# Phi by half sequences on array quarters, attention's first two tiles joined, and new ranks for the planner

## The chip, the cores and the metric

The kernel runs on one core of one Trainium2 chip. The metric is the device time of one execution in microseconds (us); lower is better. The time of the kernel before is the median of three runs, 779.21 us (779.11 to 779.4). Everything is computed in float32.

## What is computed

A transformer block over 32 sequences of 512 tokens with 256 features. The first half is an attention whose queries and keys are the same feature vector phi; the second half routes each token to the best 8 of 64 slots, updates the slots by a gated step, and reads them back. Cut to what matters:

```python
x  = x + attn(layernorm(x));  x = x + slots(layernorm(x))
# attn, per token of one sequence
q      = tanh(x @ W_charge.T + b)                    # one number per token
shell  = normalise(x @ W_shell.T + b_shell)          # 64
proj   = shell @ omega.T + rff_bias                  # 32
phi_s  = [cos(proj), sin(proj)] * scale              # 64
phi    = sum_m mag[m] * q**m * (phi_s @ W_combine[m].T)     # m = 0..4, 64 numbers
logits = phi @ phi.T * exp(-0.03 * |i - j|) / temp,  causal
out    = softmax(logits) @ (x @ W_v.T + b_v) @ W_out.T + b_out
# slots
alpha  = softmax of the 8 largest of 64 route logits, 0 elsewhere
slot   = gated step of (alpha.T @ x / sum(alpha)),  out = alpha @ (slot @ wv.T) @ wo.T
```

The decay is split into a factor that grows with the query's place (`dec_q`) and one that falls with the key's (`dec_k`), so phi is multiplied by each once and the logits come from one matrix product.

## The kernel before, in words

The work is cut into 16 groups of `GB = 2` sequences. A group has `GT = 8` tiles of 128 tokens, and its input tile `x` lies in one of five buffers. Each group passes four stages, which the code writes as functions.

- `features`: transposes of `x` (`pta`, L698), the joint projection to shell, charge and values (`pf`, L732, evicted to `sv` by L745), charges repeated over 64 columns (`qrep`, L768, GpSimd) and transposed (`ptq`), shells normalised and transposed (`pts`). The angles come from one full-array matrix product with a block-diagonal 128x128 `om` (`pp`, L858; eviction L865). After rounding (L872, L873) and the sine (L880) the powers `tp[m]` are built by multiplying with q or q squared (L891; m = 1 and 3 on VectorE, 2 and 4 on GpSimd). In `tp`, partitions 0 to 63 hold sequence 0 and 64 to 127 sequence 1, with all 512 tokens along the free axis.
- phi, the end of `features`: a 64x64 quarter of the array reads one half of the partitions and writes one half. Powers 0, 3 and 4 go through the two diagonal quarters (`STRAIGHT`, L930). Powers 1 and 2 go through the other two (`SWAPPED`, L941), and so must first stand on the other half of partitions: four DMA transfers per group on SP's queue copy `tp` to `tps` (L915). The three PE steps are chained: powers 0 and 1, then 3 and 2, then 4 alone, which occupies two quarters. Each of two PSUM banks then holds part of both sequences: ScalarE copies one bank (`both`, L958), VectorE adds the other (L962), and `dec_q` is multiplied on by VectorE (L970), `dec_k` by GpSimd (L977).
- `attention`: for each of four query tiles i, the logits of width (i+1)*128 for both sequences on the two row halves of the array (`pl`, L996), the masked minimum on VectorE (L1014), the exponential with its sum on ScalarE (L1026), the reciprocal (L1042), transposes (`ptp`, L1052), their eviction (`prT`, L1078), the product with the values (`po`, L1056), and the sum into `x` (L1065).
- `router` and `slots`: layer norm (statistics L662; the small GpSimd steps L673 to L683; application L1096), transposes `ptb`, hidden layer `ph` (L1122), logits `prr` (L1147, the two column halves of the array), transposes `prt`, eight `max`/`match_replace` pairs (L1178, L1179), the exponential (L1196), the weights `al` (L1212, GpSimd), the slots' input `psi` (L1235, column halves), the gates `prz` and `pn` (L1284), the new values `pv` (L1371), and the outputs `py` (L1391, row halves), added to `x` (L1405) and stored.

Engines take their instructions in the order in which they are emitted. That order is made by a planner (class `Plan`): each step has an engine, a cost in us, the steps it needs and the buffers it uses. `order` places the step that could start first by these costs, and among equal starts the one with the lowest rank. A rank is `g * STRIDE + (earliest time inside its group) + DELAY[stage]`. An activation table that must be loaded adds `TABLE`. The tile pools' sizes are in `SLOTS_OF`: eight PSUM banks `ps`, one `phi`, and one `tp`.

```python
STRIDE = 28.0
DELAY = {"setup": 0.0, "features": -12.0, "attention": -3.0, "router": 15.0, "slots": 15.0}
```

Of the kernel before, what the change touches and what calls it, by code (L numbers as in the profile page):

```python
# [15 lines left out]
P = 128  # L16
D = 256
KD = D // P
T = 512
NT = T // P  # L20
# [6 lines left out]
STRAIGHT, SWAPPED = (0, 3, 4), (1, 2)  # L27
# [43 lines left out]
STRIDE = 28.0  # L71

DELAY = {"setup": 0.0, "features": -12.0, "attention": -3.0, "router": 15.0, "slots": 15.0}
# [24 lines left out]
class Plan:  # L98
# [8 lines left out]
    def add(self, eng, cost, emit, after=(), uses=(), table=None, land=0.0, rank=None, spare=0):  # L107
        s = Step(eng, cost, emit, [a for a in after if a], list(uses), rank, table, land)
        s.spare = spare
        s.g, s.stage = self.group, self.stage  # L110
        for u in s.uses:
            u.users += 1
        for a in s.after:
            a.next.append(s)
        s.waits = len(s.after)
        self.steps.append(s)
        return s

    def order(self):
# [17 lines left out]
        table = None  # L137
# [6 lines left out]
        while len(placed) < len(self.steps):  # L144
            best = None
            for e, todo in ready.items():
                for s in todo:
# [13 lines left out]
                    if s.table and s.table != table:  # L161
                        key = (t + TABLE, s.rank + TABLE, s.n)
                    else:
                        key = (t, s.rank, s.n)
# [5 lines left out]
            if s.table and s.table != table:  # L170
                t, table = t + TABLE, s.table
            for u in s.uses:
                if not u.live:
                    u.live = True
                    if u.tag in slots:
                        heapq.heappop(slots[u.tag])
# [17 lines left out]
def block_kernel(ctx: ExitStack, tc: tile.TileContext, a: dict, out: bass.AP):  # L194
# [69 lines left out]
    om = const("om", [P, P])  # L264
# [181 lines left out]
    s_zero = add("DVE", 0.2, lambda: nc.vector.memset(om, 0.0), rank=-17.0)  # L446
    l_om, l_wc = [], []
    for bb in range(GB):
        r = slice(bb * SHELL, (bb + 1) * SHELL)
        for h in range(2):  # L450
            lo = bb * PHI_S + h * RFF
            l_om.append(load("POOL", om[r, lo : lo + RFF], a["omega_t"], 8, [s_zero], rank=-16.0))
# [21 lines left out]
    def magnitudes():  # L474
# [17 lines left out]
    s_di = add(  # L492
        "POOL",
        0.6,
        lambda: nc.gpsimd.iota(di(), pattern=[[1, T]], base=-(T // 2), channel_multiplier=0),
        uses=[di],
        rank=-7.0,
    )
# [218 lines left out]
    def features(g):  # L717
# [7 lines left out]
        for t in range(GT):  # L725
# [4 lines left out]
            def project(c=c, pf=pf, tiles=tiles):  # L730
                for k in range(KD):
# [28 lines left out]
        qrep = lazy("row", f"qrep_{g}", [P, NT, GB, PHI_S])  # L760
        sq = lazy("row", f"sq_{g}", [P, GT, SHELL])
        rn = small(f"rn_{g}", [P, GT])
        shn = lazy("row", f"shn_{g}", [P, NT, GB, SHELL])
        s_rep = [
            add(
                "POOL",
                0.4,
                lambda bb=bb: nc.gpsimd.tensor_copy(  # L768
                    qrep()[:, :, bb, :],
                    sv()[:, bb * NT : (bb + 1) * NT, C_Q : C_Q + 1].to_broadcast([P, NT, PHI_S]),  # L770
                ),
# [9 lines left out]
        def charges_turned():  # L781
            for c in range(NT):
                nc.tensor.transpose(
                    ptq()[:, c * P : (c + 1) * P],
                    qrep()[:, c].rearrange("p b s -> p (b s)"),
# [57 lines left out]
        def shells_turned():  # L843
# [7 lines left out]
        pp = bank(f"pp_{g}")  # L851
# [3 lines left out]
        s = add(  # L855
            "PE",
            0.86,
            lambda: nc.tensor.matmul(pp(), om, sh_t(), start=True, stop=True),  # L858
            [s, s_om],
            [pp, sh_t, ang],  # L860
        )
        s = add(
            "ACT",
            0.6,
            lambda: nc.scalar.activation(ang(), pp(), AF.Identity, bias=rffb),  # L865
            [s, s_om],
            [pp, ang],
        )
# [6 lines left out]
        s = add("DVE", 1.05, nearest, [s], [ang, turn])  # L875
# [25 lines left out]
        power("POOL", 1.2, 4, q2, s_q2)  # L901

        tps = small(f"tps_{g}", [P, len(SWAPPED), T], bufs=1)
        s_sw = {}
        for j, m in enumerate(SWAPPED):
            s_sw[m] = []
            for h in range(GB):
                to, frm = (slice(k * PHI_S, (k + 1) * PHI_S) for k in (h, 1 - h))  # L910
                s_sw[m].append(
                    add(
                        "SP",
                        0.55,
                        lambda j=j, m=m, to=to, frm=frm: nc.sync.dma_start(  # L915
                            out=tps()[to, j, :], in_=tp()[frm, m, :]
                        ),
                        [s_tp[m]],
                        [tp, tps],
                        land=2.2,  # L920
                    )
                )
        pps = [bank(f"pph_{g}_{h}") for h in range(GB)]
        phi = lazy("phi", f"phi_{g}", [P, 2, T])
        both = lazy("row", f"both_{g}", [P, T])

        def combined(straight, swapped):
            for h in range(GB):
                r = slice(h * PHI_S, (h + 1) * PHI_S)
                nc.tensor.matmul(  # L930
                    pps[h]()[h * COMB : (h + 1) * COMB, :],
                    wc[r, straight, :],
                    tp()[r, straight, :],
                    start=(straight == STRAIGHT[0]),
                    stop=(straight == STRAIGHT[-1]),
                )
            if swapped is None:
                return
            for h in range(GB):
                r = slice(h * PHI_S, (h + 1) * PHI_S)  # L940
                nc.tensor.matmul(  # L941
                    pps[h]()[(1 - h) * COMB : (2 - h) * COMB, :],
                    wc[r, swapped, :],
                    tps()[r, SWAPPED.index(swapped), :],
                    start=(swapped == SWAPPED[0]),
                    stop=(swapped == SWAPPED[-1]),
                )

        s = None
        for straight, swapped in zip(STRAIGHT, SWAPPED + (None,)):  # L950
            s = add(
                "PE",
                0.9,
                lambda straight=straight, swapped=swapped: combined(straight, swapped),
                [s_tp[straight], s_wc, s] + s_sw.get(swapped, []),
                pps + [tp, tps, phi, both],
            )
        s_a = add("ACT", 0.54, lambda: nc.scalar.copy(both(), pps[0]()), [s], [pps[0], both])  # L958
        s_b = add(
            "DVE",  # L960
            0.62,
            lambda: nc.vector.tensor_tensor(both(), pps[1](), both(), ALU.add),  # L962
            [s, s_a],
            [pps[1], both],
# [4 lines left out]
                0.6,  # L969
                lambda: nc.vector.tensor_tensor(phi()[:, 0, :], both(), dec_q, ALU.mult),  # L970
                [s_b, s_dec],
                [both, phi],
            ),
            add(
                "POOL",
                1.2,
                lambda: nc.gpsimd.tensor_tensor(phi()[:, 1, :], both(), dec_k, ALU.mult),  # L977
                [s_b, s_dec],
                [both, phi],
            ),  # L980
# [3 lines left out]
    def attention(g, sv, s_sv, phi, s_phi):  # L984
# [3 lines left out]
        for i in range(NT):  # L988
            w = (i + 1) * P
            pls = [bank(f"pl_{g}_{bb}_{i}") for bb in range(GB)]  # L990

            def logits(i=i, w=w, pls=pls):

                for bb in range(GB):
                    r = slice(bb * COMB, (bb + 1) * COMB)
                    nc.tensor.matmul(  # L996
                        pls[bb]()[:, 0:w],
                        phi()[r, 0, i * P : w],
                        phi()[r, 1, 0:w],
                        start=True,  # L1000
                        stop=True,
                    )

            s_pl = add("PE", 0.12 + 0.215 * (i + 1), logits, s_phi, pls + [phi], spare=SPARE)
            den = small(f"den_{g}_{i}", [P, GB], bufs=4)
            prs, s_ex = [], []
            for bb in range(GB):
                lg = lazy("lg", f"lg_{g}_{bb}_{i}", [P, T])
                nm = small(f"nm_{g}_{bb}_{i}", [P, 1], bufs=8)
                pr = lazy("pr", f"pr_{g}_{bb}_{i}", [P, T])  # L1010
                prs.append(pr)

                def lowest(bb=bb, w=w, pls=pls, lg=lg, nm=nm):
                    nc.vector.tensor_tensor_reduce(  # L1014
                        out=lg()[:, 0:w],
                        in0=pls[bb]()[:, 0:w],
                        in1=mask[:, T - w : T],
                        scale=1.0,
                        scalar=TOP,
                        op0=ALU.add,  # L1020
                        op1=ALU.min,
                        accum_out=nm(),
                    )

                def weights(bb=bb, w=w, lg=lg, nm=nm, pr=pr, den=den):
                    nc.scalar.activation(  # L1026
                        pr()[:, 0:w],
                        lg()[:, 0:w],
                        AF.Exp,
                        bias=nm(),  # L1030
                        scale=-1.0,
                        accum_out=den()[:, bb : bb + 1],
                    )
# [462 lines left out]
```

## Time and profile before

| | |
|---|---|
| median of three runs | 779.21 us |
| the profiled execution's own time | 780.47 us |
| its span, first to last instruction | 778.7 us |
| mean granted TensorE clock | 0.975 |
| instructions | 11783 |
| moved to and from HBM | 21.17 MB read, 16.78 MB written |

The profiled execution took 780.47 us, 1.77 us more than its span and 1.26 us more than the median of the runs. In the profile PE is TensorE's matrix products, PEld its weight loads, DVE VectorE, ACT ScalarE, POOL GpSimd and SP the queue of DMA issues. The end of a product is modelled, and products overlap, so what is read for TensorE is when instructions start. A float32 product appears as two instructions over the same columns, a transpose as one. The page has the busy time of each engine, the span in forty slices, groups of instructions by line, and the chain of work that ended last; the trace can also be asked for a timeline of single instructions and for busy times in stretches.

### The profile page before, as it was taken

How to read it: one execution, taken by the hardware profiler on the slowest of the kernel's cores; microseconds unless marked ns; L12 is line 12 of the kernel's file. 1: busy time of each engine (PE TensorE's matmuls, PEld its weight loads, DVE VectorE, ACT ScalarE, POOL GpSimd, SP SyncE). 2: the span in 40 equal slices, each digit the busy share in tenths (PEclk: the TensorE clock that was granted, in tenths of full speed). 3: DMA queues.
4: the chain of work that ended last, by engine and by line, in shares of the span. 5: the costliest groups of instructions: out<-in, count | busy, mean ns of one | idle time of the engine just before them, and what ended most of it. 6: DMA issues, size and time to landing. Idle time of an engine off the chain costs nothing.

```text
span 778.7 us, 11783 instructions
## 1 busy us (share of the span) xinstructions
PE 735.9 (95%) x3850; PEld 492.4 (63%) x3850; DVE 560.6 (72%) x1676; ACT 470.5 (60%) x963; POOL 298.5 (38%) x492
## 2 busy tenths in 40 slices
PE   5979999999999999999999999999999999999944
PEld 4646666766666666757567666767666676657522
DVE  4969647788777859787577959788587967777442
ACT  3254667747566575857576665847676665775610
POOL 7453533253333534243343543333354452231200
PEclk9998999999999999999999999999999999999965
DMA  7531010040302113130402113040311211020111
GB/s 207 183 114 49 1 28 0 8 129 21 116 2 82 54 28 109 28 109 1 136 2 82 55 29 109 5 132 2 90 47 46 90 28 55 8 75 2 55 54 55
DMA packets 44749, 47.11 MB, mean 60 GB/s; under 512 B 4848, under 2 KB 39760, under 8 KB 44688
## 3 DMA queue, kind: packets, MB, share of 16 engines
q1 hardware_dynamic: 42816, 45.40, 19.0%
q10 hardware_dynamic: 1376, 0.62, 0.3%
q8 instruction: 31, 0.51, 0.3%
q0 software_dynamic: 496, 0.33, 0.2%
q14 instruction: 30, 0.25, 0.1%
HBM read 21.17 MB, written 16.78 MB: 49 GB/s over the span
## 4 chain that ended last, share of the span: by engine, by line
PE 82%; DVE 6%; ACT 4%; POOL 2%; DMA 2%; issue 1%; SPq 1%; ACTq 0%; POOLq 0%; DVEq 0%
PE pf L732 17%; PE po L1056 16%; PE ph L1122 6%; PE pph L930 5%; PE pl L996 5%; PE ptp L1052 4%; PE prz L1284 4%; PE psi L1235 4%; PE py L1391 4%; PE ptb L698 3%; PE pta L698 3%; PE pv L1371 2%; PE prr L1147 2%; PE pp L858 2%; PE pn L1284 2%
## 5 line engine op out<-in xcount | busy, mean ns | idle before, releaser
L1056 PE MATMUL po<-sv,prT 128*128 128x256 f32 x640 | 150.8, 379 | 0.6 <-ACT prT L1078 0.6
L732 PE MATMUL pf<-wf,xT 128*128 128x321 f32 x512 | 143.3, 435 | 0.6 <-DVE wf L372 0.6
L1056 PEld LDWEIGHTS po<-sv,prT 128*128 128x128 f32 x640 | 115.8, 189 | 16.7 <-issue 1.9
L732 PEld LDWEIGHTS pf<-wf,xT 128*128 128x128 f32 x512 | 95.2, 189 | 45.2 <-issue 6.0
L1065 DVE SCALAR_TENSOR_TENSOR x<-po,den,x 128x256 f32<-128x256 f32 x128 | 60.7, 478 | 35.3 <-PE po L1056 34.1
L1026 ACT ACTIVATE pr<-lg,nm 128x128 f32<-128x128 f32 (+3 forms) x128 | 71.2, 561 | 23.0 <-DVE nm L1014 22.7
L891 POOL TENSOR_TENSOR tp<-tp,q 128x512 f32<-128x512 f32 x32 | 49.5, 1548 | 77.5 <-ACT tp L880 76.3
L1078 ACT COPY prT<-ptp 128x128 f32<-128x128 f32 (+3 forms) x128 | 51.2, 427 | 38.5 <-PE ptp L1052 38.4
L1096 ACT ACTIVATE xm<-x,lnb 128x256 f32<-128x256 f32 x128 | 65.8, 594 | 11.1 <-POOL lnb L683 11.1
L977 POOL TENSOR_TENSOR phi<-both,dec_k 128x512 f32<-128x512 f32 x16 | 27.7, 1731 | 113.5 <-DVE both L962 106.5
L745 DVE SCALAR_TENSOR_TENSOR sv<-pf,lna,bias_f 128x321 f32<-128x321 f32 x128 | 63.2, 541 | 10.2 <-PE pf L732 10.0
L1014 DVE CUSTOM_DVE_ANT_0 lg<-pl,mask 128x128 f32<-128x128 f32 (+3 forms) x128 | 57.4, 485 | 10.5 <-PE pl L996 6.2
L710 ACT COPY xmT<-ptb 128x512 f32<-128x512 f32 x64 | 34.9, 594 | 41.0 <-PE ptb L698 41.0
L1122 PE MATMUL ph<-xmT,w1x 128*128 128x512 f32 x128 | 59.4, 595 | 0.2 <-ACT xmT L710 0.2
L1405 DVE TENSOR_TENSOR x<-py,x 128x512 f32<-128x512 f32 x64 | 39.9, 683 | 27.1 <-PE py L1391 27.1
L662 DVE BATCH_NORM_STATS2 bnb<-x 128x6 f32<-128x256 f32 x128 | 52.5, 422 | 2.4
L662 DVE BATCH_NORM_STATS2 bna<-x 128x6 f32<-128x256 f32 x128 | 46.5, 411 | 8.7 <-DMA x<-in_x_dram 8.7
L996 PE MATMUL pl<-phi 64*128 64x128 f32 (+3 forms) x256 | 47.7, 482 | 5.2 <-POOL phi L977 5.1
L1052 PE MATMUL ptp<-ident,pr 128*128 128x128 f32 x320 | 49.6, 274 | 0.3 <-DVE x L1065 0.3
L1052 PEld LDWEIGHTS ptp<-ident,pr 128*128 128x128 f32 x320 | 38.7, 140 | 16.9 <-issue 5.6
L930 PE MATMUL pph<-tp,wc 64*64 64x512 f32 x192 | 47.7, 606 | 0.0
L1330 POOL TENSOR_TENSOR nn<-nn,rh 128x256 f32<-128x256 f32 x16 | 11.8, 736 | 91.9 <-DVE rh L1321 65.8
(177 smaller groups left out, 1401.9 us busy)
## 6 DMA issues: line engine op xcount, KB each, us to landing
x<-in_x_dram SPq DMA_DIRECT2D x32, 512.0 KB, 4.4
out_dram<-x SPq DMA_DIRECT2D x64, 256.0 KB, 2.5
tps<-tp SPq DMA_DIRECT2D x64, 128.0 KB, 2.3
setup<-in_gru_whh_t_dram SPq DMA_DIRECT2D x1, 768.0 KB, 7.9
wih<-in_gru_wih_t_dram SPq DMA_DIRECT2D x1, 768.0 KB, 9.0
setup<-in_W_v_dram ACTq DMA_DIRECT2D x1, 256.0 KB, 6.2
setup<-in_W_out_t_dram ACTq DMA_DIRECT2D x1, 256.0 KB, 7.0
setup<-in_gru_bih_dram SPq DMA_DIRECT2D x1, 256.0 KB, 8.0
```

What stands on the lines that cost most here:

```text
L662: lambda t=t: nc.vector.bn_stats(st()[:, t, :], src()[:, t, :]),
L732: nc.tensor.matmul(pf()[:, 0:NF], tiles[k]()[:, c * P : (c + 1) * P], wf[:, k, :], start=(k == 0), stop=(k == KD - 1),)
L745: lambda t=t, pf=pf: nc.vector.scalar_tensor_tensor(sv()[:, t, :], pf()[:, 0:NF], ln()[:, 1, t : t + 1], bias_f, ALU.mult, ALU.add,),
L930: nc.tensor.matmul(pps[h]()[h * COMB : (h + 1) * COMB, :], wc[r, straight, :], tp()[r, straight, :], start=(straight == STRAIGHT[0]), stop ...
L996: nc.tensor.matmul(pls[bb]()[:, 0:w], phi()[r, 0, i * P : w], phi()[r, 1, 0:w], start=True, stop=True,)
L1014: nc.vector.tensor_tensor_reduce(out=lg()[:, 0:w], in0=pls[bb]()[:, 0:w], in1=mask[:, T - w : T], scale=1.0, scalar=TOP, op0=ALU.add, op1= ...
L1026: nc.scalar.activation(pr()[:, 0:w], lg()[:, 0:w], AF.Exp, bias=nm(), scale=-1.0, accum_out=den()[:, bb : bb + 1],)
L1052: nc.tensor.transpose(pt()[:, j : j + P], prs[bb]()[:, j : j + P], ident)
L1056: nc.tensor.matmul(po()[:, 0:D], pr_t()[:, j * P : (j + 1) * P], sv()[:, bb * NT + j, C_V:NF], start=(j == 0), stop=(j == i),)
L1065: nc.vector.scalar_tensor_tensor(xt()[:, t, :], po()[:, 0:D], den()[:, bb : bb + 1], xt()[:, t, :], ALU.mult, ALU.add,)
L1096: lambda t=t: nc.scalar.activation(xm()[:, t, 0:D], xt()[:, t, :], AF.Identity, bias=ln()[:, 4, t : t + 1], scale=ln()[:, 1, t : t + 1],),
L1122: nc.tensor.matmul(ph(), w1x[:, k, :], tiles[k](), start=(k == 0), stop=(k == KD - 1))
```

## The change

- The planner counts a change of the way the array is divided: a TensorE step whose `split` differs from that of the step placed before it has its rank raised by `SWITCH = 2.0` in the choice. Steps of `pp`, `pph`, `pl`, `prr`, `psi` and `py` carry their division; others have none.
- `STRIDE` goes from 28 to 26 and all four delays fall, by different amounts.
- The charges are repeated in another order (four copies of half the width instead of two), so that from `ptq` on each half of partitions holds half of the tokens of both sequences: columns 0 to 255 sequence 0 and 256 to 511 sequence 1, with the halves of sequence 1 exchanged.
- `om` is 128x64 without zeros. `pp` is four products of 256 columns, one on each quarter, into two banks, evicted by two instructions.
- phi is one TensorE step that needs all five powers: five times four products of 256 columns, one on each quarter, added up in PSUM. Bank h holds one half of the tokens of both sequences, with the sequence on the partition half. The swap transfers, the copy and the sum of `both` are gone. Four VectorE products of 128x256 write phi from PSUM, two with `dec_q` and two with `dec_k`; GpSimd does none.
- Sequence 1 has its token halves exchanged in phi, so the decay tiles are made with that exchange (three `iota` instead of one), and `logits` addresses phi by `at(bb, token)`, in pieces of at most 256 keys.
- In `attention`, query tiles 0 and 1 are one step: one bank of width 384 per sequence, one set of transposes, one eviction, one `po` bank for two tiles, one reciprocal.

The diff, cut to its core:

```diff
-STRIDE = 28.0
-DELAY = {"setup": 0.0, "features": -12.0, "attention": -3.0, "router": 15.0, "slots": 15.0}
+SWITCH = 2.0
+STRIDE = 26.0
+DELAY = {"setup": 0.0, "features": -32.0, "attention": -14.0, "router": -1.0, "slots": 3.0}
...
                     if s.table and s.table != table:
                         key = (t + TABLE, s.rank + TABLE, s.n)
+                    elif e == "PE" and s.split != split:
+                        key = (t, s.rank + SWITCH, s.n)
...
+        def projected():
+            for h in range(2):
+                for bb in range(GB):
+                    r = slice(bb * SHELL, (bb + 1) * SHELL)
+                    lo = (h ^ bb) * HT
+                    nc.tensor.matmul(
+                        pps[bb]()[h * PHI_S : (h + 1) * PHI_S, 0:HT],
+                        om[r, :],
+                        sh_t()[r, lo : lo + HT],
+                        start=True, stop=True,
+                    )
...
-        tps = small(f"tps_{g}", [P, len(SWAPPED), T], bufs=1)
...
-                        lambda j=j, m=m, to=to, frm=frm: nc.sync.dma_start(
-                            out=tps()[to, j, :], in_=tp()[frm, m, :]
-                        ),
...
-        for straight, swapped in zip(STRAIGHT, SWAPPED + (None,)):
-            s = add("PE", 0.9, ..., [s_tp[straight], s_wc, s] + s_sw.get(swapped, []), ...)
-        s_a = add("ACT", 0.54, lambda: nc.scalar.copy(both(), pps[0]()), ...)
-        s_b = add("DVE", 0.62, lambda: nc.vector.tensor_tensor(both(), pps[1](), both(), ALU.add), ...)
+        def combined():
+            for m in range(ORDER + 1):
+                for bb in range(GB):
+                    for h in range(2):
+                        r = slice(h * PHI_S, (h + 1) * PHI_S)
+                        nc.tensor.matmul(
+                            phs[h]()[bb * COMB : (bb + 1) * COMB, 0:HT],
+                            wc[r, m, :],
+                            tp()[r, m, bb * HT : (bb + 1) * HT],
+                            start=(m == 0), stop=(m == ORDER),
+                        )
+        s = add("PE", 2.3, combined, list(s_tp.values()) + [s_wc], phs + [tp, phi], split="64x64")
         s_phi = [
+            add("DVE", 0.42, lambda ...: nc.vector.tensor_tensor(
+                    phi()[:, n, h * HT : (h + 1) * HT], phs[h]()[:, 0:HT],
+                    dec[:, h * HT : (h + 1) * HT], ALU.mult), [s, s_dec], [phs[h], phi])
+            for h in range(2)
+            for n, dec in enumerate((dec_q, dec_k))
         ]
...
-        for i in range(NT):
+        for tiles in ((0, 1), (2,), (3,)):
+            off = {i: P * sum(j + 1 for j in tiles if j < i) for i in tiles}
+            width = P * sum(i + 1 for i in tiles)
...
+                for i in tiles:
+                    for lo in range(0, (i + 1) * P, HT):
+                        w = min(HT, (i + 1) * P - lo)
+                        for bb in range(GB):
+                            r = slice(bb * COMB, (bb + 1) * COMB)
+                            q, k = at(bb, i * P), at(bb, lo)
+                            nc.tensor.matmul(pls[bb]()[:, off[i] + lo : off[i] + lo + w],
+                                phi()[r, 0, q : q + P], phi()[r, 1, k : k + w], ...)
```

## The prediction

> **What bounds the kernel now.** I read the page's busy times and slices first, then the stretches, then the timeline of TensorE and the chain.
>
> ```profile
> PE 735.9 (95%) x3850; PEld 492.4 (63%) x3850; DVE 560.6 (72%) x1676; ACT 470.5 (60%) x963; POOL 298.5 (38%) x492
> ...
> PE   5979999999999999999999999999999999999944
> ...
> PEclk9998999999999999999999999999999999999965
> ```
>
> TensorE is busy except in the first tenth and the last twentieth; no other engine passes 72%. The stretches say the same of the middle and the end (after the stretch and its length, the columns are PE, PEld, DVE, ACT, POOL, clock):
>
> ```profile
> 330.00:380.00 50.00, 49.87 (x279) 32.59 (x279) 34.54 (x106) 32.77 (x69) 21.74 (x39) 1.00 0.19 56
> ...
> 740.00:760.00 20.00, 8.88 (x36) 4.58 (x33) 8.48 (x33) 2.87 (x4) 1.04 (x1) 0.60 0.15 52
> ```
>
> The modelled ends hide small gaps, so I time TensorE by starts:
>
> ```profile
> 376.76 0.65 PE L930 MATMUL pph<-tp,wc 64*64 64x512 f32 x2
> 376.77 0.65 PE L941 MATMUL pph<-tps,wc 64*64 64x512 f32 x2
> 377.24 0.59 PE L930 MATMUL pph<-tp,wc 64*64 64x512 f32 x2
> ```
> ```profile
> 421.66 2.00 PE L1391 MATMUL py<-val,alT 64*128 64x256 f32 x16
> 423.59 0.66 PE L1153 MATMUL prt<-ident,rlT 128*128 128x128 f32 x4
> ```
> ```profile
> 415.22 3.62 PE L1056 MATMUL po<-sv,prT 128*128 128x256 f32 x16
> 418.67 1.03 PE L1371 MATMUL pv<-wov,hnT 128*128 128x256 f32 x4
> ```
>
> Sixteen `po` products of 256 columns take 418.67 - 415.22 = 3.45, so 0.216 each. The four quarter products of a `pph` round start 0.01 apart and the next such round 0.43 to 0.48 later: four quarters cost what one costs, 0.43 for 512 columns. `py` needs 1.93 for eight rounds of two; 8 x 0.216 = 1.73, so **a change of the array's division costs about 0.2**; the same sum for four `pph` rounds (378.64 - 376.76 = 1.88, less 1.72) gives 0.16. I use 0.17.
>
> Work of one group by these rates: 72 transposes x 0.11 = 7.9; 32 `pf` of 321 columns x 0.27 = 8.6; 22 rounds of 512 columns outside `pl` x 0.43 = 9.4; 66 rounds of 256 x 0.216 = 14.3 (`po` 40, `py` 8, `psi` 8, gates and values 8, `pl` 2); `pl`'s other widths 1.7; sum 41.9. In the order of the compiled program the division changes 13 to 14 times per group, 2.3 more: 44.2. The chain has `psi` of two groups at 305.02 and 393.83, so a group takes 44.4. Nothing is left over: the middle is TensorE's own work, and only what shortens this work counts there. Two ends remain. At the start:
>
> ```profile
> 59.68 4.64 PE L996 MATMUL pl<-phi 64*128 64x128 f32 x16 [5.14 <-POOL phi L977]
> ```
>
> At the end, the last `po` runs from 716.49 to 720.1, and the other 58.6 us are the last groups' chain through four engines (on the chain `al` at 750.48, `psi` at 751.58, `prz` at 757.27).
>
> **What the Trainium skill says.** "TensorEngine Tiling (Array Packing)", Key Properties: tiles work independently, and changing the division drains TensorE. The trace agrees: starts 0.01 apart, and 0.16 to 0.2 per change. The same page, Gotcha 1: different row tiles may not use the same PSUM bank at once. The new code gives each row half its own bank (`phs[h]`, `pps[bb]`), as the old one did. "TensorE: Matmul & The Clock Gate", the table under Why this matters for your kernels: an idle gap over some 3 us sends the clock back to half. After the 5.14 gap the sixteen `pl` took 4.64, against 2.76 in a later group (0.42, 1.28 and 1.06 on the chain), and the clock of 740 to 760 is 0.60.
>
> **The change, part by part.**
>
> *phi on quarters (TensorE, on the path).* Before: four rounds with four quarters busy and two for power 4 with only two, 6 x 0.43 = 2.57. After: 40 instructions in 10 rounds x 0.216 = 2.16. Saved 0.41. *Angles:* 2 x 0.43 = 0.86 become 2 x 0.216 = 0.43. Saved 0.43, if a quarter round of 256 columns costs 0.216. No row shows one. Half of the 512-column quarter round is the low bound; the high bound is four weight loads one after another, 4 x 0.13 = 0.54. The loads of a round start 0.02 apart in the trace, so I take 0.216. *Logits:* the same columns in 12 rounds instead of 8: +0.01. *Divisions:* 201 runs before, 199 after over the whole program, since `pp` adds changes and the ranks join others: -0.3 in all. Sum: 0.83 x 16 + 0.3 = **-13.6**.
>
> *Other engines (off the path in the middle).* VectorE loses `both` and `phi` (0.68 + 0.69) and gets four products of 128x256 from PSUM; the nearest row is `val`, 0.42: +0.3 per group, less a reciprocal of 0.16. ScalarE loses 0.58 (`both`), gains 0.05 to 0.17 (an eviction in two), and its `prT` copies of 0.26 and 0.38 per sequence become one of 0.48: -0.8. GpSimd loses 1.73 and gets four copies instead of two at 0.43: 0 to +0.85. SP loses 64 transfers, so that loads of `x` no longer stand behind transfers that wait for powers. VectorE becomes some 36 of 43 us and remains second; this costs nothing while TensorE leads. If it led, it would cost its 0.2 per group, 3 us.
>
> *Start.* Before, `pph` ended at 53.94, ScalarE's copy at 55.2, but VectorE added at 57.10, because statistics of a later `x` stood ahead waiting for their transfer; then `dec_k` on GpSimd, 1.78, and `pl` at 59.68. In the new order phi's four products (1.7) stand ahead of such statistics. The second `x` is loaded ahead of nine small transfers, so the first weights' copies no longer stand behind its arrival at 18.0, and the slow 3.3 reciprocal (L513) stands behind two `sv`. I work out `qrep` and the first sine 1.5 to 2 earlier, the last power at 48.8 instead of 50.7, phi at 52.9, `pl` at about 53.3 with no gap and full clock. But the second group's single phi step now stands before the first `ptp` and waits for its powers, two times 1.72 on GpSimd after a sine near 54.8: it starts at 58.3 and ends at 60.6, against 67.6 before. Of these 7, 1.7 is the TensorE saving of two groups, counted above: **-5.2**. If TensorE again waits there, 0; if all follows, -7.
>
> *Ranks.* In the middle the distances in TensorE's order between a producer and its reader stay above what the chains need: weights `prt` to `psi` 12.1 us of queued work at least (12.6 before), `prr` to `prt` 1.9 (2 to 3), `pph` to `pl` 3.9 (7.4, but with a chain shorter by 1.5). I allow **+1** for the tight ones. Near the end `prt` of group 13 to its `psi` has only 8.2, and rl, eight max pairs, the exponential behind eight `xm`, the sums and `al` need about 11: **+2** before the last `po`. Behind the last `po` stand 29.4 us of queued work instead of 27, so 2.4 moves from before it into a stretch with idle time: **-2.4**. In that stretch the weights of group 15 come no later than before (31.7 after the last `po`, before 31.5), but `pv` and `py` of group 14 now stand between `psi` and `prz` of group 15, in part at half clock: **+1.4**.
>
> Sum: -13.6 - 5.2 + 1 + 2 - 2.4 + 1.4 = -16.8. The profiled span 778.7 becomes 761.9, with 1.77 around it 763.7; the median lies 1.26 under the profiled execution, so **762.4**.
>
> **The rivals.** *Quarters in line.* If loads or banks let only two quarters run together, phi takes 20 rounds x 0.216 = 4.3, +1.75 per group against 2.57, and the angles stay at 0.86: +28 instead of -13.3, about 804, **slower**. It decides from a round of 0.31 (16.8 / (16 x 12 rounds) above 0.216). Against it: four starts 0.01 apart with the same quarters and banks. For it: twice the weight loads per time. *New waits eat the gain.* The lower delays pack the chains closer; if in each group one reader waits 0.6, +10 and 772. For it: the shorter distances above; against it: shorter phi chain, less ScalarE and GpSimd work. *Only the sum of work counts.* Start and end give nothing: 779.2 - 13.6 = 765.6. *Ends do better:* the start yields 7, the end's +2 and +1.4 vanish, some 755.
>
> **How the numbers follow.** Forecast 762.4, itself 758 to 767, 0.55; only the sum 0.17; new waits 0.13; better ends 0.08; quarters in line or another loss 0.07. The range 752 to 772 takes in all but the last and the upper half of the waits. Faster by over 0.2% (about what measurement can tell from no change) is 0.92, within it 0.02, slower 0.06.
>
> **What would show it.** `psi` of two groups 87 apart (43.5 each, from 88.8); rounds of `pph` 0.216 apart with four starts each; no TensorE wait over 1 us between 130 and 650; the first `pl` near 53 and clock 1 there; the last `po` near 702, then 60 to the end. Rounds of 0.3 or more, a group over 44, or `pl` again near 60 would make it wrong.

## The result, and the profile after

The changed kernel takes 766.26 us (median of four runs, 764.55 to 767.33) against 779.29 for the kernel before beside it: a ratio of 0.983, 95% interval 0.981 to 0.985. The profiled execution took 766.67 us with a span of 764.6, 14.1 less than before.

The page of the changed kernel (busy time and share by engine, then slices of 19.1 us):

```profile
PE 719.9 (94%) x4394; PEld 510.5 (67%) x4394; DVE 559.1 (73%) x1691; ACT 446.8 (58%) x920; POOL 268.7 (35%) x510
...
PE   3998999999999999999999999999999999989844
...
PEclk9999999999999999999999999999999999999876
```

TensorE is busy 16 us less, VectorE about as long as before. The third slice (38 to 57), at 7 tenths before, is full now; the first fell from 5 to 3, and near the end two slices fell from 9 to 8. The stretches of the changed kernel (columns as in the prediction) say the same:

```profile
330.00:380.00 50.00, 50.00 (x304) 35.63 (x305) 41.34 (x124) 31.62 (x69) 19.68 (x37) 1.00 0.13 43
740.00:760.00 20.00, 14.12 (x64) 8.53 (x60) 8.16 (x17) 1.79 (x4) 1.44 (x2) 0.76 0.17 60
```

The timeline of TensorE of the changed kernel has the disputed rounds (start, length, instruction):

```profile
54.65 2.44 PE L1004 MATMUL pl<-phi 64*128 64x128 f32 x24
...
216.85 0.66 PE L889 MATMUL pp<-shT,om 64*64 64x256 f32 x8
217.44 1.12 PE L1326 MATMUL prz<-wih,giT 128*128 128x512 f32 x2
...
402.05 2.39 PE L951 MATMUL pph<-tp,wc 64*64 64x256 f32 x40
404.37 1.35 PE L1087 MATMUL po<-sv,prT 128*128 128x256 f32 x5
```

Read from start to start: forty instructions of phi occupy 404.37 - 402.05 = 2.32, which is ten rounds of 0.216 and one change of division (0.16). The eight of the angles occupy 0.59: two rounds of 0.216 and 0.16. The first `pl` starts at 54.65 instead of 59.68, without a gap ahead of it.

**A balance.** To see where 14.1 us went, I split each span in three. *Work*: the columns of every TensorE instruction at 0.216 per 256, divided by the number of such instructions that the array's division lets run at once (the lone pair of power 4 in the old code counts as if it filled the array, since half of it could not be used). *Divisions*: the number of runs of one division in the trace, times 0.17. *Rest*: what is left, that is waits, half clock and empty time; it is also given by stretches.

| us | span | work | divisions | rest | rest to 216 | 216 to 660 | 660 to the end |
|---|---|---|---|---|---|---|---|
| before | 778.7 | 679.3 | 34.1 | 65.3 | 27.9 | 1.6 | 35.8 |
| changed | 764.6 | 665.4 | 33.9 | 65.3 | 23.7 | 1.2 | 40.4 |
| difference | -14.1 | -13.9 | -0.2 | 0 | -4.2 | -0.4 | +4.6 |

In both kernels only 1 to 2 of 444 us in the middle are not explained by work and divisions; so the rates hold. The whole gain is the work. What the start won, the end lost: from the end of the last `po` to the end of the span it was 58.6 before and is 64.7 now.

### The profile page after: what moved, and what is told of

It reads as the page before. It is cut to its first block, busy times and chain, and to the rows that moved or that the text cites. A ratio compares the mean times of both kernels' runs of the same rounds, so it can differ in the third digit from the quotient of the medians.

```text
span 764.6 us, 12620 instructions
## 1 busy us (share of the span) xinstructions
PE 719.9 (94%) x4394; PEld 510.5 (67%) x4394; DVE 559.1 (73%) x1691; ACT 446.8 (58%) x920; POOL 268.7 (35%) x510
## 4 chain that ended last, share of the span: by engine, by line
PE 88%; DVE 5%; DMA 2%; ACT 2%; issue 1%; POOL 1%; POOLq 0%; DVEq 0%; ACTq 0%
PE pf L753 18%; PE po L1087 18%; PE ph L1164 7%; PE pl L1004 5%; PE ptp L1081 5%; PE pph L951 4%; PE psi L1277 4%; PE prz L1326 4%; PE py L1433 4%; PE ptb L719 3%; PE pta L719 3%; PE prr L1189 2%; PE pv L1413 2%; DMA x<-in_x_dram 2%; PE pn L1326 2%; DVE rest L1221 1%
## 5 line engine op out<-in xcount | busy, mean ns | idle before, releaser
L1087 PE MATMUL po<-sv,prT 128*128 128x256 f32 x640 | 149.2, 380 | 0.7 <-DVE nm L1033 0.7
L1099 ACT COPY prT<-ptp 128x384 f32<-128x384 f32 (+1 forms) x96 | 47.8, 515 | 49.4 <-PE ptp L1081 49.3
L1033 DVE CUSTOM_DVE_ANT_0 lg<-pl,mask 128x128 f32<-128x128 f32 (+3 forms) x128 | 57.6, 486 | 25.1 <-PE pl L1004 23.5
L1116 DVE SCALAR_TENSOR_TENSOR x<-po,den,x 128x256 f32<-128x256 f32 x128 | 58.1, 476 | 23.5 <-PE po L1087 22.6
L932 POOL TENSOR_TENSOR tp<-tp,q 128x512 f32<-128x512 f32 x32 | 46.8, 1462 | 69.5 <-ACT tp L921 68.3
L1164 PE MATMUL ph<-xmT,w1x 128*128 128x512 f32 x128 | 62.1, 611 | 0.0
L683 DVE BATCH_NORM_STATS2 bnb<-x 128x6 f32<-128x256 f32 x128 | 48.1, 415 | 1.1
L789 POOL COPY qrep<-sv 128x128 f32<-128x128 f32 x64 | 18.2, 303 | 85.6 <-DVE sv L766 85.4
L1447 DVE TENSOR_TENSOR x<-py,x 128x512 f32<-128x512 f32 x64 | 39.9, 682 | 7.5 <-PE py L1433 7.5
L1004 PE MATMUL pl<-phi 64*128 64x256 f32 (+1 forms) x384 | 45.3, 362 | 0.0
L731 ACT COPY xT<-pta 128x512 f32<-128x512 f32 x64 | 34.3, 596 | 14.5 <-PE pta L719 14.5
L951 PE MATMUL pph<-tp,wc 64*64 64x256 f32 x640 | 38.9, 382 | 1.6 <-DVE tp L932 1.1
## 6 DMA issues: line engine op xcount, KB each, us to landing
setup<-in_gru_whh_t_dram SPq DMA_DIRECT2D x1, 768.0 KB, 4.9
wih<-in_gru_wih_t_dram SPq DMA_DIRECT2D x1, 768.0 KB, 7.5
```

The source lines that it names most:

```text
L683: lambda t=t: nc.vector.bn_stats(st()[:, t, :], src()[:, t, :]),
L951: nc.tensor.matmul(phs[h]()[bb * COMB : (bb + 1) * COMB, 0:HT], wc[r, m, :], tp()[r, m, bb * HT : (bb + 1) * HT], start=(m == 0), stop=(m ...
L1004: nc.tensor.matmul(pls[bb]()[:, off[i] + lo : off[i] + lo + w], phi()[r, 0, q : q + P], phi()[r, 1, k : k + w], start=True, stop=True,)
L1033: nc.vector.tensor_tensor_reduce(out=lg()[:, c], in0=pls[bb]()[:, c], in1=mask[:, T - w : T], scale=1.0, scalar=TOP, op0=ALU.add, op1=ALU.min,
L1087: nc.tensor.matmul(po()[:, d * D : (d + 1) * D], pr_t()[:, lo : lo + P], sv()[:, bb * NT + j, C_V:NF], start=(j == 0), stop=(j == i),)
L1116: nc.vector.scalar_tensor_tensor(xt()[:, t, :], po()[:, d * D : (d + 1) * D], den()[:, d, bb : bb + 1], xt()[:, t, :], ALU.mult, ALU.add,)
```

## The experiments

All times are medians; the kernel before took 778.9 to 779.2 beside them. phi_twice and phi_halves leave the planner's order as it is. Each of the other edits also changes the order that the planner makes, so such a run shows the edit together with its order. The balance of all of them (profiled spans, same columns):

| us | span | work | divisions | rest to 216 | 216 to 660 | 660 to the end |
|---|---|---|---|---|---|---|
| changed | 764.6 | 665.4 | 33.9 | 23.7 | 1.2 | 40.4 |
| phi_twice | 795.7 | 700.1 | 33.8 | 19.3 | 1.1 | 41.4 |
| phi_halves | 784.5 | 665.4 | 33.8 | 28.3 | 14.4 | 42.6 |
| old_ranks | 768.0 | 665.3 | 34.2 | 25.1 | 7.1 | 36.3 |
| old_ranks_unjoined | 772.9 | 665.4 | 38.0 | 26.9 | 4.1 | 38.5 |
| new_ranks_old_code | 807.7 | 679.3 | 36.0 | 33.6 | 18.1 | 40.7 |
| tail_router_first | 756.2 | 665.4 | 33.5 | 23.3 | 1.1 | 32.9 |
| unjoined_tail | 771.7 | 665.4 | 35.5 | 22.8 | 9.0 | 39.0 |
| no_switch_tail | 762.7 | 665.4 | 35.3 | 26.6 | 0.7 | 34.7 |
| x1_later | 762.5 | 665.4 | 32.8 | 22.8 | 1.6 | 39.9 |
| tail_and_x1 | 756.4 | 665.5 | 32.4 | 22.8 | 1.3 | 34.4 |
| switch4_tail | 756.7 | 665.4 | 30.5 | 23.2 | 2.5 | 35.1 |
| switch4_middle | 753.1 | 665.4 | 30.1 | 22.4 | 2.0 | 33.2 |

### What a round of four quarters costs

**phi_twice.** Twice the products, in the same banks. The second ten begin the sum anew (`start=(m == 0)`), so phi is computed twice and not doubled, as the text below has it; what is measured is the time of the products.

```diff
-            for m in range(ORDER + 1):
+            for m in list(range(ORDER + 1)) * 2:
```

> The changed kernel with the twenty phi products issued twice into the same banks (twice the sum, so phi is doubled; nothing else moves in the order). Theory, that a round of four quarter products of 256 columns costs 0.216 and lies on the path in full: 10 x 0.216 x 16 = 34.6 more, 799 to 803. Rival, that the queue of weight loads sets the round under load: 0.31 or more per round, 816 or above. Rival, that part of phi's time is hidden in waits of TensorE: under 796.

Measured: 797.33, 31.1 more. TensorE's timeline of this kernel:

```profile
417.02 4.55 PE L951 MATMUL pph<-tp,wc 64*64 64x256 f32 x80
421.50 2.86 PE L1087 MATMUL po<-sv,prT 128*128 128x256 f32 x12
```

Eighty instructions take 4.48, against 2.32 for forty: 2.16 for ten rounds, 0.216 each. The first `po` of groups 4 to 12 go from 222.2 to 568.7 in the changed kernel, 43.3 per group, and from 228.5 to 592.3 here, 45.5: all of it on the path. The missing 3.5 of 34.6 are at the start, where the rest falls by 4.4: there TensorE had waited anyway, and the first `po` of the first two groups come as before (63.9 and 87.6, against 64.0 and 87.7). So the first theory holds in the middle, and the rival of phi hidden in waits holds for the first two groups.

**phi_halves.** The same forty instructions, in another order.

```diff
-            for m in range(ORDER + 1):
-                for bb in range(GB):
-                    for h in range(2):
+            for h in range(2):
+                for m in range(ORDER + 1):
+                    for bb in range(GB):
```

> The changed kernel with the twenty phi products of a group emitted by row half (all ten of one half, then all ten of the other) instead of four quarters in turn; the same products and results. Theory, that TensorE starts products in the order given, so that only two quarters of one row half can run together: 20 rounds x 0.216 instead of 10, as much as the doubled phi, 795 to 801. Rival, that a product on a free quarter overtakes those queued for a busy one: 766, as the changed kernel.

Measured: 786.43 (ratio to before 1.010, 1.0075 to 1.012): 20.2 more than the changed kernel, so slower than before, and between the two theories.

```profile
411.69 3.73 PE L951 MATMUL pph<-tp,wc 64*64 64x256 f32 x40
415.36 2.86 PE L1087 MATMUL po<-sv,prT 128*128 128x256 f32 x12
```

3.67 instead of 2.32: 16.2 rounds, neither 20 nor 10. The single starts show why: ten pairs follow each other by 0.21 from 411.69 to 413.69, and a second series of ten pairs begins at 413.05, when three pairs (six instructions) of the first have not started. The trace doesn't name the row half; that the second series is the other half follows from the order in which the products are written. So the gain of the quarters hangs on that order.

### What the ranks are worth

**old_ranks** and **new_ranks_old_code** exchange the planner's numbers of the two kernels. The edit of old_ranks follows; new_ranks_old_code has the reverse for `STRIDE` and `DELAY`, without `SWITCH`.

```diff
-SWITCH = 2.0
-STRIDE = 26.0
-DELAY = {"setup": 0.0, "features": -32.0, "attention": -14.0, "router": -1.0, "slots": 3.0}
+SWITCH = 0.0
+STRIDE = 28.0
+DELAY = {"setup": 0.0, "features": -12.0, "attention": -3.0, "router": 15.0, "slots": 15.0}
```

> The new code with the planner's old numbers (STRIDE 28, the old four delays, no counted division changes). Theory, that the gain is TensorE's own work in phi and the angles and the ranks are worth little: a group in the middle takes 43.4 us again, the transfer of the second x goes back behind the small loads, and behind the last po the order of before comes back (58.6 us to the end). In all about 764, between 760 and 767. Rival, that the gain needs the new ranks: TensorE waits in the middle of each group for phi, a group takes 44 or more, and the time is 770 or above.

> The code of before with the new STRIDE and delays alone (division changes not counted, since the code has no place for that). Theory, that the ranks bring nothing without the new phi: the distance from pph to pl in TensorE's order gets shorter while the old chain through ScalarE, VectorE and GpSimd does not, and behind the last po the slow order of the changed kernel appears; 212 division runs instead of 201 cost another 2 us. 780 to 788, and 64 us or more from the last po to the end. Rival, that the ranks carry part of the gain: 770 to 776, with the last po at 712 or earlier.

Measured: 770.05 (ratio to before 0.986 to 0.990) and 812.35 (1.039 to 1.043). Both expectations missed the size. With the new code, the new ranks save 5.9 of waits in the middle and 1.4 at the start, and lose 4.1 at the end, together 3.8 in the medians. The time of old_ranks is that of my rival, its mechanism is not: a group still takes 43.4 (groups 4 to 12), and TensorE's list of waits from 216 to 660 does not name phi. It names `ptb` waiting for VectorE's `sv` (3.4 in five waits) and `ptq` for GpSimd's `qrep` (0.5, once). The list counts a wait from the modelled end of the product before it and so falls short of the 7.1 of the balance. Behind the last `po` it has 54.6, not 58.6. With the old code the new ranks cost 33 in the medians and 29 in the profiled span. The end isn't the reason: it has 60.5 behind the last `po`, where I had expected 64 or more. In the middle of that kernel, five groups from 372 to 604, the list of waits has one entry (total, times, longest):

```profile
PE ptp L1052 <- DVE val L1379: 8.2, 5, 1.6
```

and its timelines of TensorE and VectorE show what it is:

```profile
449.49 1.03 PE L1371 MATMUL pv<-wov,hnT 128*128 128x256 f32 x4
...
453.46 0.44 PE L1052 MATMUL ptp<-ident,pr 128*128 128x128 f32 x2 [1.63 <-DVE val L1379]
```
```profile
452.13 0.21 DVE L1179 MATCH_REPLACE8 rest<-top,rl 128x64 f32<-128x64 f32 x1
452.37 0.69 DVE L1187 TENSOR_TENSOR rl<-rl,top 128x512 f32<-128x512 f32 x1
452.98 0.42 DVE L1379 TENSOR_TENSOR val<-pv,bias_s 128x256 f32<-128x256 f32 x1
```

`ptp` reads nothing that `val` writes, and its exponentials had ended by 448.8. What it can wait for there is the PSUM bank that `val` empties, and `val` stands behind eight max pairs (448.0 to 452.3). So it isn't the wait for phi that I had expected. That it is the bank is argued from this; no run changed the number of banks.

### What the joined tiles are worth

```diff
-        for tiles in ((0, 1), (2,), (3,)):
+        for tiles in ((0,), (1,), (2,), (3,)):
```

**unjoined_tail** has this edit on tail_router_first (below), **old_ranks_unjoined** on old_ranks.

> Attention's first two query tiles taken apart again (four steps of pl instead of three), on top of the kernel with the last group's router first (758.3). Theory, that joining saves only work off the path (one reciprocal and two evictions per group) and TensorE's columns are the same: the order has 209 division runs instead of 197, worth 2, so 759 to 762. Rival, that the short first tile's own chain makes TensorE wait in each group, so that joining carries part of the gain: 765 or above.

> The new phi and angles alone: attention's first two tiles apart as before, and the planner's old numbers (STRIDE 28, old delays, no counted division changes). Theory, that joining removes waits of TensorE only where the new ranks pack the chains close (it was worth 15.5 there): as with the old numbers and joined tiles, 768.5 to 772. Rival, that joining removes waits in every group whatever the ranks: 776 or above.

Measured: 773.82, 15.5 more than tail_router_first, and 775.20 (0.994 to 0.997 of before), 5.2 more than old_ranks. Both ranges of my theories were missed. Joining, with the order that goes with it, is part of the gain, not work off the path. Of the 15.5, 2.0 are divisions, 7.9 rest in the middle and 6.1 rest at the end (less 0.5 at the start). The waits of TensorE from 216 to 660, of which the changed kernel has none in this list:

```profile
PE po L1091 <- ACT prT L1103: 3.5, 3, 1.4
PE pph L955 <- POOL tp L936: 0.8, 3, 0.3
PE py L1437 <- DVE val L1425: 0.3, 1, 0.3
```

Its 4.6 fall short of the 7.9 as above. `po` and `pph` wait three times each, not in every group, as the rival had it. At the end, `py` waits 3.0 more for `val` than in tail_router_first; the other 3.1 there I did not trace.

With the old numbers, 3.8 of the 5.2 are divisions: each extra `pl` step is a run of its own (224 runs against 201). The start and the end have 1.8 and 2.2 more rest, and the middle even has 3.0 less. My theory, that joining matters only with close ranks, is half right: the waits in the middle come only with these, the divisions with either numbers. No run joined the tiles with the old phi.

The corner old_ranks_unjoined is also the change's first part alone, new phi and angles without joining and ranks. It saves 3.8 in the medians (5.8 in the span), though its work is 13.9 less: 3.9 went into 23 more division runs, 2.5 into waits of the middle and 2.7 into the end, and only 1.0 came at the start.

### What a division change is worth

**no_switch_tail** has `SWITCH = 0.0` on tail_router_first, **switch4_tail** has `SWITCH = 4.0`.

> SWITCH = 0 on top of the kernel with the last group's router first (758.3). Theory, that a counted division change is worth only what the change itself costs TensorE: the compiled order has 208 division runs instead of 197, 11 x 0.17 = 1.9, so 759.5 to 761.5. Rival, that the raised rank also keeps steps of one kind together and so spaces the chains: over 763; or that the changes are hidden in waits: 758.3 within 0.7.

> SWITCH = 4 instead of 2 on top of the kernel with the last group's router first (758.3): the order has 180 division runs instead of 197. Theory, that a run less saves its 0.17 wherever nothing else changes: 17 x 0.17 = 2.9, so 754.5 to 757. Rival, as with SWITCH 0, that runs count for little and what counts is which waits the other order makes: 758 or above.

Measured: 762.54 and 758.24, against 758.32 for tail_router_first. Here the theory of 0.17 per run fails as a forecast of the total: with 0, the median rises by 4.2 and the span by 6.5, of which 1.8 are divisions, 3.3 waits at the start and 1.8 at the end, where the order is another; a group still takes 43.4. With 4, it holds in the middle: 108 runs from 220 to 660 instead of 127, which is 1.9 less per group, and a group takes 42.98 instead of 43.31, so 0.17 per run. Waits of the middle and the end (1.4 and 2.2 more) give the 3.0 of divisions back.

### Start and end

**x1_later** puts the load of the second `x` back behind the nine small loads.

```diff
-                load("SP", dst, ..., 512, after, [xs[g]])
+                load("SP", dst, ..., 512, after, [xs[g]], rank=43.0 if g == 1 else None)
```

> The changed kernel with the load of the second group's x put back behind the nine small loads (rank 43, as its rank was before). Theory, that this load early on takes transfer time from the weights and puts its statistics ahead on VectorE: the first pw near 13.5 instead of 16.7, the first pf near 18 instead of 21.2, the last power and the first pl 1 to 2.5 us earlier (52 to 53.5), 763 to 765 in all. The compiled order also has 193 division runs instead of 199, worth 1 us at most. Rival, that the loss at the start is made good by waits later, before the first po: the first po stays at 64, and the time at 766.

VectorE and TensorE of the changed kernel, then TensorE of this one:

```profile
14.97 0.43 DVE L683 BATCH_NORM_STATS2 bna<-x 128x6 f32<-128x256 f32 x1 [6.39 <-DMA x<-in_x_dram]
15.31 0.67 DVE L362 TENSOR_REDUCE wv_mean<-setup 128x2 f32<-128x512 f32 x1
```
```profile
14.89 1.12 PE L448 MATMUL pm<-wf,onesD 128*128 128x65 f32 x4 [5.71 <-POOL onesD L332]
16.67 3.78 PE L376 MATMUL pw<-setup 128*128 128x256 f32 x8 [0.66 <-DVE setup L365]
...
21.19 3.14 PE L753 MATMUL pf<-wf,xT 128*128 128x321 f32 x11
```
```profile
13.38 1.12 PE L449 MATMUL pm<-wf,onesD 128*128 128x65 f32 x4 [4.36 <-POOL onesD L333]
14.30 3.72 PE L377 MATMUL pw<-setup 128*128 128x256 f32 x8
...
19.11 5.31 PE L754 MATMUL pf<-wf,xT 128*128 128x321 f32 x18
...
52.08 2.69 PE L1005 MATMUL pl<-phi 64*128 64x128 f32 x24
```

In the changed kernel VectorE waits 6.39 for an `x` with the mean of the first weights (L362) queued behind it. With the later load, `pw` starts 2.4, `pf` 2.1 and the first `pl` 2.6 earlier. VectorE is only a part of this: 1.5 of the 2.4 stand already at `pm`, which waits for the ones (`onesD`) that GpSimd writes behind its small loads (at 14.62, and here at 13.10). The first `po` comes at 57.4 instead of 64.0, but of the gain the balance keeps 0.9 by 216. With 1.1 of divisions the span falls by 2.1. The median falls by 1.1 to 765.19, which the runs can't tell from no change (764.3 to 766.3, against 764.6 to 767.3): the earlier start is shown by the traces, a shorter time is not.

**tail_router_first** lowers the rank of the last group's router.

```diff
                 s.rank = s.g * STRIDE + s.at + DELAY[s.stage]
+                if s.g == 15 and s.stage == "router":
+                    s.rank -= 20.0
```

> The changed kernel with the ranks of the last group's router lowered by 20, so that prr and prt of group 15 stand before prz and pn of group 14 and the eight xm of group 15 before the exponential of group 14; everything up to the last po stays. Theory, that the 64.7 us behind the last po come from this order: prt of group 15 some 4 to 5 us earlier, its psi 33 to 34 us behind the last po instead of 38.6, the end 57 to 60 us behind it, 759 to 762 in all. Rival, that the end is one chain that only changes places (group 14's work takes the same time wherever it stands, in part at half clock): 64 us again, 765 to 767.

Measured: 758.32 (0.970 to 0.974), 8 less and 0.7 below the range of the theory, and the span behind the last `po` is 56.9 instead of 64.7. TensorE and ScalarE of the changed kernel, the last `po` having ended at 699.9:

```profile
710.73 1.82 PE L719 MATMUL ptb<-ident,xm 128*128 128x128 f32 x6 [2.32 <-ACT xm L1138]
712.35 3.62 PE L1164 MATMUL ph<-xmT,w1x 128*128 128x512 f32 x4
...
716.75 1.96 PE L1277 MATMUL psi<-xm,al 128*64 128x257 f32 x16
718.64 1.98 PE L1164 MATMUL ph<-xmT,w1x 128*128 128x512 f32 x4
...
722.40 1.98 PE L1326 MATMUL prz<-wih,giT 128*128 128x512 f32 x4
...
725.09 0.60 PE L1195 MATMUL prt<-ident,rlT 128*128 128x128 f32 x4
...
738.55 2.96 PE L1277 MATMUL psi<-xm,al 128*64 128x257 f32 x16
```
```profile
704.97 3.06 ACT L1138 ACTIVATE xm<-x,lnb 128x256 f32<-128x256 f32 x6 [1.96 <-POOL lnb L704]
708.17 1.28 ACT L1238 ACT_TABLE_LOAD   x1
709.46 0.72 ACT L1238 ACTIVATE rl<-rl,rtau 128x512 f32<-128x512 f32 x1
710.09 1.08 ACT L1138 ACTIVATE xm<-x,lnb 128x256 f32<-128x256 f32 x2
```

And TensorE of tail_router_first, whose last `po` ended at 699.4:

```profile
711.96 1.98 PE L1168 MATMUL ph<-xmT,w1x 128*128 128x512 f32 x4 [0.97 <-ACT xmT L735]
...
718.59 0.66 PE L1199 MATMUL prt<-ident,rlT 128*128 128x128 f32 x4 [0.45 <-ACT rlT L1207]
...
730.44 3.27 PE L1281 MATMUL psi<-xm,al 128*64 128x257 f32 x16
```

In the changed kernel the exponential of group 14 and its table load (2.0) stand between the sixth and the seventh `xm` of group 15, TensorE waits 2.32 and goes on at half clock (four `ph` in 3.41, not 1.72), and `psi` of group 14 stands ahead of group 15's second `ph`, `prz` and `pn` ahead of its `prt`. At half clock `ptb`, `ph` and `pta` take some 3 longer (an estimate from their starts: 6.0 from 710.73 to 716.75, where the full rates give 2.8). Then all that follows `prt` (max pairs, exponential, sums, weights) is late: `psi` of group 15 starts 38.6 behind the last `po`. With its router first, `prt` stands 19.2 instead of 25.2 behind it and `psi` 31.1, and group 14's gates (719.1 to 721.8) fill a wait that was there anyway. By that estimate half of the 6.0 that `prt` gains is the half clock, and half the order. The rival, one chain that only changes places, is out.

**tail_and_x1** and **switch4_middle** join what helped. In the latter, `SWITCH` is 4 for the groups up to 12.

> Both edits at once on the changed kernel: the last group's router first and the second x loaded behind the small loads. If they act on separate ends and add up (8.0 and 1.1), 757.2, between 756 and 758.5. If the gain at the start is taken back before the middle, 758.3 as with the tail alone.

> SWITCH = 4 for the groups up to 12 and 2 for the last three, on top of the kernel with the last group's router first (758.3); behind the last po the order is that kernel's. Theory, that the fewer division runs saved 0.33 per group in the middle (42.98 against 43.31 with SWITCH = 4 throughout) and that the loss at the end came from the other order there: 754.5 to 756.5, with 57 us behind the last po. Rival, that the last groups are bound by their own chains and take back what the middle gains: 758 again.

Measured: 758.29, so the earlier start gives nothing beside the repaired end (the rest at the end is 1.5 higher: the clock granted from 676.5 to 679.8 was 0.50, and `ptb` and `ph` there take 5.67 where tail_router_first needs 4.28), and 755.23 (0.967 to 0.971). The last is the fastest version: 24 less than before, 11 less than the changed kernel. It keeps the cheaper middle (43.01 per group) and 57 behind the last `po`.

## Why the prediction held, point by point

- **phi, angles and divisions, -13.6: right.** Measured -14.1 in the balance. A quarter round costs 0.216, the low end of the bounds; phi_twice shows it on the path. Two slips of the sums change nothing: the round that decides against the quarters is 0.30, not 0.31 (0.216 + 16.8 / 192), and the 7 of the start less 1.7 are 5.3. The rival of quarters in line is out for this order; phi_halves shows that it was a matter of writing: at 16.2 rounds it comes to 786, slower than before. No run let both row halves write one PSUM bank, so what the prediction takes from the skill on banks was not tried.
- **Start, -5.2: right in kind, 1 too large.** Measured -4.2. The gap ahead of `pl` is gone (54.65, forecast 53.3; 53.94, which the prediction calls the end of `pph`, is the start of its last pair) and the second group's phi ends at 61.0, as forecast (60.6). Wrong was the step of "`qrep` and the first sine 1.5 to 2 earlier": I took the early second `x` as a help, while it made VectorE wait 6.39 and GpSimd's ones come 1.5 later, and the last power came at 51.7 instead of 48.8. x1_later shows it: with the later load the last power comes at 49.0.
- **Ranks in the middle, +1: wrong by little.** Measured -0.4. But the step beneath it was wrong: I costed the ranks as a small loss and the joined tiles at +0.01 on the path. The runs show that the new code with old ranks waits 5.9 more in the middle, and unjoined tiles with new ranks 7.9 more. "Nothing is left over" in the old middle was true (1.6 of 444); that the new code would keep this by itself was not. That the forecast met the middle although two of its costs were far off is luck: all three parts came together, and nothing in the prediction says that they had to.
- **The end, +2 - 2.4 + 1.4 = +1: the term that was mis-sized.** Measured +4.6, and the sum hides a larger miss. From 660 to the last `po` the rest is 3.6 before and 3.5 now: the +2 did not come. Behind the last `po` it is 32.2 before and 36.9 now: +4.7, where -2.4 + 1.4 = -1 was forecast. The step that failed is "the weights of group 15 come no later than before (31.7 after the last `po`)": they fed `psi` at 38.6. I had seen `pv` and `py` of group 14 between `psi` and `prz` of group 15, but not that its exponential split the `xm`, nor that `psi` stood ahead of the second `ph`, and `prz` and `pn` ahead of `prt`, nor the half clock after the wait for `xm`. tail_router_first undoes this and wins 7.5 there.
- **Signs.** A group takes 43.3 (forecast 43.5), the rounds of `pph` are 0.216 apart, no wait over 1 us stands between 130 and 650, and the last `po` ends at 699.9 (forecast 702), with 64.7 behind it (forecast 60). `psi` of two groups 87 apart was a bad sign to choose: in the new order they lie unevenly (295.5, 336.4, 379.1, 426.9).

The terms missed by +1.0 (start), -1.4 (middle), +3.6 (end) and -0.5 (work and divisions): together 2.7, the difference between the spans of 761.9 and 764.6. The median was missed by 3.9 (766.3 for 762.4), since the profiled execution took 2.07 more than its span, not 1.77, and the median lies 0.4 below it, not 1.26. Nearest to the measured time was the rival that only the sum of work counts (765.6), but not for its reason: start and end did not give nothing, they gave -4.2 and +4.6, which happen to cancel.

## What to carry to other kernels

Split the span into work at measured rates, division changes and rest before costing a change: a saving of work counts in full only as long as the rest stays where it is, and a planner's numbers fit one code (the same new ranks were worth -3.8 with the new phi and joined tiles, and +33 with the old code). When work is pushed behind the last big step, write down the order of the last two groups on every engine, and put the last group's longest chain first. Where parts of the array run at once, write the instructions so that neighbours use different parts.

## What the hardware showed unexpectedly

- In phi_halves, products on a free row half started while three pairs written ahead of them on the busy half had not. The Trainium skill, "TensorE: Matmul & The Clock Gate", Part 3 under The mechanism, says that matmuls start and end in program order; the starts of this trace differ from it, and the measurement decides here. The sentence ahead of the prediction, that engines take their instructions in the order in which they are emitted, has this exception on TensorE.
- The page "TensorEngine Tiling (Array Packing)", Key Properties, gives no price for the drain at a change of division. Here it is 0.16 from phi's 2.32, and 0.17 from 0.33 us and 1.9 runs less per group in switch4_tail.
- After small waits for `xm` and one of 2.32, shorter than the 3 us that the prediction quotes, the clock granted from 709.9 to 716.7 was 0.50 in the changed kernel, and four `ph` took 3.41, half speed. In tail_router_first, where the longest wait there was 0.97, it was 1.00 from 705 to 726, and the same four are listed with 1.98 instead of 3.62.
- The length of one wait does not decide this alone. A wait of 2.35 ahead of the same sixteen `ptb` (near 675) was followed by 0.50 in tail_and_x1 and by 1.00 in tail_router_first and in the changed kernel. What decides between them stays open.
